# Layer 0's aggregate of panel 3: five of its seven products split a second time

## The chip, the cores and the metric

The kernel runs on one core of a Trainium2 chip. The metric is the device time of one execution in microseconds (us); the time given for a kernel is the median of several executions.

## What is computed

A graph with 2708 nodes of 1024 features goes through two attention layers. Cut to what matters here:

```
h = relu(layernorm(x))
# layer 0
f, g      = h @ Wf + bf, h @ Wg + bg
attention = softmax(where(adj > 0, relu(f @ g.T), NEG), axis=1)
x         = x + attention @ (h @ W + bW)
# layer 1: scores are leaky_relu(f1 + f2.T), the rest is alike
h         = relu(layernorm(x))
x         = x + relu(attention @ (h @ W))
```

All of it is in float32. The kernel forms `h.T @ attention.T` first (the aggregate, 1024 features by the nodes of a panel) and multiplies by W after that (the projection).

## The kernel before

**Panels.** The columns of the transposed attention are cut into five panels of 576, 576, 532, 512 and 512 nodes. The loop from L1768 on takes them one after the other through layer 0: `scores` (L1400) forms a panel's exponents' arguments, `project_q` (L701) prepares the right side of the next panel's scores, `aggregate` (L924) multiplies the rows of h by the panel's attention, and `project` (L1250) multiplies that by W. For the last two panels the order is shifted: the projection of panel 3 comes after the scores of panel 4 and before panel 4's aggregate. The loop from L1908 does the same in layer 1.

**The aggregate as seven products.** The 20 full row tiles are 10 pairs (`NQ`). Left and right side are seen as 2 by 2 blocks (the feature halves; the two tiles of a pair; the two halves of the panel), and seven block products M1 to M7 with sums of blocks on both sides take the place of eight. The left sums of layer 0 lie in DRAM as `hg_d` (made in `rows_h` and `sums_h`, L368 and L376); those of layer 1 lie in `hr_d` (`pair_h`). The right sums are made on VectorE in place: `T1`, `second`, `fourth` (L932 to L949). Each product is 40 matmuls of a 128x128 left block by half a panel, in `accumulate` (L665); in the trace each shows as two instructions, so 80 in all. The order is M1, M5, M2, M6, M3, M7, M4. The two left-over row tiles (`MONO`, `TINY`) have no partner and are added by `left_over` (L965) three times and by `into_m15` (L977) once.

**Split once more.** In layer 1, panels 1 to 4 use `aggregate_quartered` (L1087): each of the seven products is itself split into seven, over two pairs of tiles (`NK` = 5) and a quarter of the panel, so it becomes seven small products of 20 matmuls of 128x128 by a quarter panel. Their left sums of sums lie in `hs2_d`; `put_quarters` (L406) makes them: it reads 512 KB, makes four VectorE subtractions and additions of 256 columns, and writes 512 KB back. Their right sums are made by `make` (L1054): 20 VectorE instructions for one product, into five `quarter` tiles. The order is M1, M5, M2, M6, M7, M3, M4. A small product reads a `hc2` tile of 512 KB; two `hl2` tiles of 512 KB hold the last quarter-row of a product. The last small product of each product, M4 (`left_out`), is put off until after the first small product of the next.

**What sets the order of the work.** Loads go out on SyncE's queue in program order (`load`, L137). Stores and the reads of `put_quarters` go out on GpSimd's queue. VectorE work that isn't urgent is put into lists (`put`, L201): `later`, and `lazy` for work that only layer 1 needs. `behind(us)` (L214) is called at fixed places among the matmuls; it adds credit and takes items from `later`, and if that is empty and `spare[0]` is set also from `lazy`, until the credit is used up. An item's first number is what it costs in credit. When an item is taken, the loads of the next ones are put out too (`ahead`, L206). `spare[0]` is set during layer 0's aggregates of panels 1 to 4 (L1789), so layer 1's left sums of sums are made there. `accumulate` calls `behind(3.0)` four times in each product. What is not `held` is placed by the compiler's scheduler, which may move it among its engine's instructions.

**Where things are kept.** The pool `slots` has 54 buffers of up to 576 columns of float32: the panel's 22 attention tiles, the 14 tiles of the next panel's right side (`B`), `T1`, `quarter`, masks, the running maxima `mx` and others. The pool `strm` has 12 buffers of 4 KB for each partition: all tiles loaded on the fly (`hc`, `hc2`, `hl2`, `hq`, `As`, `w`, `adj_i`). [...] After the last product of an aggregate, GpSimd scales the result by the inverse sums (`scale`, L1019); the quartered form does it on VectorE (L1140).

Of the kernel before, what the change touches and what calls it, by code (L numbers as in the profile page):

```python
# [57 lines left out]
def kernel(  # L58
# [82 lines left out]
    def store(o, i):  # L141
        for a, b in in_16(o, i):
            nc.gpsimd.dma_start(a, b)  # L143
# [7 lines left out]


    hs_d = [dram.tile([P, 8, NH, P], FP, name=f"hs_d{q}") for q in range(NQ)]
    groups = [[q, q + 1] for q in range(0, NQ, 2)]
    group_of = {q: (i, j) for i, g in enumerate(groups) for j, q in enumerate(g)}
    assert sorted(group_of) == list(range(NQ))
    hg_d = [dram.tile([P, 7, len(g), W], FP, name=f"hg_d{i}") for i, g in enumerate(groups)]
    NK = NQ // 2
    WH = W // 2
    hr_d = dram.tile([P, 7, 2, 2, NK, WH], FP, name="hr_d")  # L160
    hs2_d = dram.tile([P, 7, 4, NK, WH], FP, name="hs2_d")

    def rows_at(m, q):

# [38 lines left out]

    def one(of=None):
        of = later if of is None else of
        for it in of[:4 if of is lazy and from_slots[0] else ahead[0]]:  # L206
            if it[1]:
                it[1]()
                it[1] = None
        us, _, go = of.pop(0)[:3]  # L210
        go()
        return us
# [154 lines left out]

    def rows_h(q, ha, hb):  # L368

        i, j = group_of[q]  # L370
        for m, h in ((M1, ha[0]), (M5, ha[1]), (M2, hb[0]), (M4, hb[1])):
            store(hg_d[i][:, m, j], h)

    summed, sums_may = [0], [True]

    def sums_h():  # L376

        def fetch(q, two):
            i, j = group_of[q]
            for m in (M1, M2):  # L380
                two.append(stream("hr", (P, 2, W)))
                (load if "m" in got else by_scalar)(two[-1], hg_d[i][:, m:m + 2, j])

        def first(q, two):
            (a0, a1), (b0, b1) = ((t[:, 0], t[:, 1]) for t in two)
            add(b1, a1, b1)
            sub(a1, a0, a1)

        def second(q, two):
            (a0, a1), (b0, b1) = ((t[:, 0], t[:, 1]) for t in two)  # L390
            sub(a0, b1, a0)
            sub(b0, b0, a0)
            i, j = group_of[q]
            store(hg_d[i][:, M6:M7 + 1, j], two[0])
            store(hg_d[i][:, M3, j], b0)
            store(hg_d[i][:, M5, j], b1)
            summed[0] += 1
        for q in range(NQ):
            two = []
            put(1.4, lambda q=q, two=two: held(first, q, two), lambda q=q, two=two: fetch(q, two), ready=lambda: sums_may[0])  # L400
            put(1.4, lambda q=q, two=two: held(second, q, two), ready=lambda: sums_may[0])

    BY_QUARTERS = (M1, M5, M2, M6, M7, M3, M4)
    made_quarters = {}

    def put_quarters(m, k, to=lazy):  # L406

        two = []

        def fetch():  # L410
            if from_slots[0]:
                two.extend(slot(f"hq{h}", (P, 2, WH)) for h in range(2))
            else:
                t = stream("hq", (P, 4, WH))
                two.extend(t[:, 2 * h:2 * h + 2] for h in range(2))
            for h in range(2):
                nc.gpsimd.dma_start(two[h], hr_d[:, m, h, :, k])

        def go():
            a11, a12, a21, a22 = (two[h][:, i] for h in range(2) for i in range(2))  # L420
            add(a22, a21, a22)
            sub(a21, a11, a21)
            sub(a11, a22, a11)
            sub(a12, a12, a11)
            for h in range(2):
                store(hs2_d[:, m, 2 * h:2 * h + 2, k], two[h])
            made_quarters[m] = made_quarters.get(m, 0) + 1
        put(1.7, go, fetch, to=to)

    def quarters_until(m):  # L430
        while made_quarters.get(m, 0) < NK:
            one(lazy if lazy else later)

    u = consts.tile([P, NC], FP, name="u")
# [489 lines left out]
    def aggregate(l, p, S, sm, then={}, rate=3.0):  # L924
# [26 lines left out]
        hc = {}  # L951

        order_of_products = (M1, M2, M4, M5, M6, M3, M7) if first else (M1, M5, M2, M6, M3, M7, M4)
        steps = [(m, i) for m in order_of_products for i in range(len(groups))]

        def left(m, q, d):
            i, j = group_of[q]
            at = steps.index((m, i))
            for m_, i_ in steps[at:at + (3 if l else 1)]:
                if (m_, i_) not in hc:  # L960
                    hc[m_, i_] = stream("hc", (P, 4, WH) if l else (P, 2, W))
                    load(hc[m_, i_], hr_d[:, m_, :, :, i_].rearrange("p h f c -> p (h f) c") if l else hg_d[i_][:, m_])
            return hc[m, i][:, d // 2 * 2 + j, d % 2 * P:(d % 2 + 1) * P] if l else hc[m, i][:, j, d * P:(d + 1) * P]

        def left_over(ps, e, s, start=False):  # L965
# [68 lines left out]
    def quarters_of(p, S):  # L1034
# [47 lines left out]
        def fourth():  # L1082
            for q in range(NQ):
                sub(t1(q), wb_(q)[:, lo], wa_(q)[:, lo])
        return {"make": make, "right": right, "first": first, "fifth": fifth, "second": second, "fourth": fourth}

    def aggregate_quartered(p, S, sm, of_right, then={}, fine=1.2):  # L1087

# [7 lines left out]
        lasts = {}  # L1098

        def product(m, n, ps, start):  # L1100
            quarters_until(m)
            if (m, 0) not in lasts:
                for i, of in enumerate((hr_d[:, m, :, :, NK - 1].rearrange("p h f c -> p (h f) c"), hs2_d[:, m, :, NK - 1])):
                    lasts[m, i] = stream("hl2", (P, 4, WH))
                    load(lasts[m, i], of)
            t = stream("hc2", (P, NK - 1, WH))
            raw = n in (M1, M2, M4)
            i = {M1: 0, M2: 1, M4: 3, M6: 0, M3: 1, M7: 2, M5: 3}[n]
            load(t, hr_d[:, m, i // 2, i % 2, :NK - 1] if raw else hs2_d[:, m, i, :NK - 1])
            last = lasts[m, int(not raw)][:, i]  # L1110
            for k in range(NK):
                for d in range(2):
                    lhs = t[:, k] if k < NK - 1 else last
                    nc.tensor.matmul(ps[:, d], lhs[:, d * P:(d + 1) * P], inner_right(m, n, k),  # L1114
                                     start=(start and k == 0 and d == 0), stop=(k == NK - 1), skip_group_check=True)
            behind(fine)
# [4 lines left out]
        def left_over(banks, e, s, fresh):  # L1121

            two = stream("hl", (P, W + 2 * P))
            load(two, hgl_d[1][:, e])
            cols = lambda b: slice(s.start + b * hb, s.start + (b + 1) * hb)
            for (a, b), ps in banks.items():
                for d in range(2):
# [41 lines left out]
        def with_second():  # L1169
# [2 lines left out]

        before_next = {M1: lambda: make(M5), M5: with_second, M2: lambda: (of_right["fourth"](), make(M6)), M6: lambda: make(M7),
                       M7: lambda: make(M3), M3: lambda: make(M4)}
        left_out = None
        for m in BY_QUARTERS:
            V = [quad(*direct[m])[:, 2 * r:2 * r + 2] for r in range(2)] if m in direct else [v[:, :, :h] for v in in_pairs("V")]
            c11, c12 = (V[0][:, :, b * hb:(b + 1) * hb] for b in range(2))
            c21, c22 = (V[1][:, :, b * hb:(b + 1) * hb] for b in range(2))
            X = bank2("gx")  # L1180
# [35 lines left out]
                into_place(m, V, 1)  # L1216
                scale(m, 1)
            if m == M5:
                of_right["second"]()
            if m == M5:  # L1220
                inverse.append(inverse_sums(p, sm))
            if m in then:
                then[m]()
        left_out()
# [354 lines left out]
    def rows_done(t, xt):  # L1579
# [14 lines left out]
        if panel_of[t] == NP - 1:  # L1594
# [18 lines left out]
            else:  # L1613
# [14 lines left out]
                (held if last else call)(rest[0])  # L1628
                put_max(1, q)
                if q == NQ - 1:  # L1630
                    for m in BY_QUARTERS:
                        put_quarters(m, q // 2, later)
                    for p in range(2, NP):
                        for s in (NQ - 2, NQ - 1):
                            put_max(p, s, lazy)
# [11 lines left out]
        if whole and q == LEFT:  # L1647
            put(0.0, lambda: left_h(1, *(done_rows[s] for s in mine)))
            put(0.0, met)
        elif whole:  # L1650
            put(2.7, lambda: pair_h(q, *(done_rows[s] for s in pairs[q])))
            put(0.0, met)
            quads_met[q // 2] = quads_met.get(q // 2, 0) + 1
            if quads_met[q // 2] == 2:
                put(0.0, lambda: [put_quarters(m, q // 2) for m in BY_QUARTERS])

    def halves_of_tiny(name):
        t = slot(name)[:, :2 * P].rearrange("p (e j) -> p e j", e=2)
# [7 lines left out]
        return list(full(p)) + ([MONO, TINY][p - 1:p] if p in (1, 2) else [])  # L1666

    ORDERED = (NP - 1,)

    def by_gpsimd(o, i, **k):  # L1670
        tc.keep_in_program_order(nc.gpsimd.dma_start(o, i, **k))
# [96 lines left out]
    for p in range(NP):  # L1768
# [18 lines left out]
            then[M6] = lambda: first_masks(NP - 1, 1)  # L1787
            then[M7] = lambda: first_masks(NP - 1, 2)
        spare[0], from_slots[0] = p > 0, p == NP - 1  # L1789
        G[p] = aggregate(0, p, S, got["sm"], then)  # L1790
        spare[0] = False
        if p == 0:
            flush()
            ahead[0] = 2
            for s in range(1, NP):
                columns_to_row(r_d[s], s, r_[:, first_col[s]:])
            spread_wa()
# [110 lines left out]
    for p in range(NP):  # L1908
# [3 lines left out]
            then = dict(zip((M2, M6) if p else (M3, (M7, "middle")), (lambda p=p: take_shifts(p + 1), lambda p=p: take_weights(p + 1))))  # L1912
        spare[0] = p < 2
        ahead[0] = 2 if p else 4
        g = aggregate_quartered(p, S, sm, next_right, then, fine=1.0) if p else aggregate(1, p, S, sm, then, rate=4.0)
        hooks = {}
        if p + 1 < NP:
            next_right = quarters_of(p + 1, got["P"][0])
# [31 lines left out]
```

## Time and profile before

| what | us |
|---|---|
| median of 3 executions | 3048.35 (3043.93 to 3048.83) |
| the profiled execution | 3049.19 |
| its span | 3047.3 |
| TensorE matmul busy | 2993.9 |
| TensorE weight load busy | 2294.2 |
| VectorE busy | 2047.6 |
| ScalarE busy | 536.8 |
| GpSimd busy | 496.9 |
| DMA | 766.78 MB, mean 252 GB/s |

All times of single instructions come from that one profiled execution, on a clock that starts with its span. PE is TensorE's matmul, PEld its weight load, DVE is VectorE, ACT ScalarE, POOL GpSimd, SP SyncE, SPq SyncE's DMA queue. Names such as `hc<-hg_d` are output and input of an instruction, with buffer numbers left out (so `hs_d` stands for `hs_d` and `hs2_d`, `hc` for `hc` and `hc2`, `hl` for `hl` and `hl2`). Almost all VectorE instructions have line L45, that of a helper. An instruction's duration overlaps with the next one's start, so a pace is read from the difference of two starts. Times in parentheses or brackets after a row are the idle time before it and what ended it.

### The profile page before, as it was taken

How to read it: one execution, taken by the hardware profiler on the slowest of the kernel's cores; microseconds unless marked ns; L12 is line 12 of the kernel's file. 1: busy time of each engine (PE TensorE's matmuls, PEld its weight loads, DVE VectorE, ACT ScalarE, POOL GpSimd, SP SyncE). 2: the span in 40 equal slices, each digit the busy share in tenths (PEclk: the TensorE clock that was granted, in tenths of full speed). 3: DMA queues.
4: the chain of work that ended last, by engine and by line, in shares of the span. 5: the costliest groups of instructions: out<-in, count | busy, mean ns of one | idle time of the engine just before them, and what ended most of it. 6: DMA issues, size and time to landing. Idle time of an engine off the chain costs nothing.

```text
span 3047.3 us, 41722 instructions
## 1 busy us (share of the span) xinstructions
PE 2993.9 (98%) x14642; PEld 2294.2 (75%) x14642; DVE 2047.6 (67%) x4667; ACT 536.8 (18%) x880; POOL 496.9 (16%) x770
## 2 busy tenths in 40 slices
PE   8998999999999999999999999999999999999999
PEld 4576777667877588885888886784767959879695
DVE  5776794585742686616965276867878768887863
ACT  4420020020200121101210111302232121212200
POOL 1421111210112110223111111131212010020201
PEclk9999999999999999999999999999999999999999
DMA  6989878887466786768957588679768768878887
GB/s 232 302 271 272 311 276 308 264 286 235 133 236 165 228 273 195 247 156 251 292 188 251 179 241 258 223 292 335 245 212 264 263 202 299 294 265 297 264 294 268
DMA packets 392704, 766.78 MB, mean 252 GB/s; under 512 B 65728, under 2 KB 206944, under 8 KB 392464
## 3 DMA queue, kind: packets, MB, share of 16 engines
q1 hardware_dynamic: 332336, 584.80, 59.6%
q0 software_dynamic: 54464, 164.78, 16.1%
q10 hardware_dynamic: 5696, 14.55, 1.4%
q8 instruction: 116, 1.90, 0.2%
q14 instruction: 92, 0.75, 0.1%
HBM read 630.04 MB, written 138.11 MB: 252 GB/s over the span
## 4 chain that ended last, share of the span: by engine, by line
PE 73%; DVE 11%; issue 8%; DMA 5%; POOL 1%; ACT 1%; SPq 1%; POOLq 0%; DVEq 0%; ACTq 0%
PE sz L1425 6%; PE gy L679 6%; PE gz L679 6%; PE gz L1114 5%; PE gx L679 5%; PE sx L1425 4%; PE pz L1314 4%; PE sy L1425 4%; PE px L1314 4%; PE py L1314 3%; PE gy L1114 3%; PE gx L1114 3%; PE gv L679 3%; PE M_ps L591 3%; PE qz L679 2%
## 5 line engine op out<-in xcount | busy, mean ns | idle before, releaser
L1425 PE MATMUL sz<-B,As 128*128 128x288 f32 (+2 forms) x1200 | 292.0, 392 | 6.0 <-DVE st L45 5.1
L1425 PEld LDWEIGHTS sz<-B,As 128*128 128x128 f32 x1200 | 227.2, 190 | 55.2 <-DVE st L45 8.4
L1425 PE MATMUL sx<-B,As 128*128 128x288 f32 (+2 forms) x800 | 200.8, 394 | 12.4 <-DMA As<-hs_d 10.4
L1425 PE MATMUL sy<-B,As 128*128 128x288 f32 (+2 forms) x800 | 199.0, 392 | 0.0
L1425 PEld LDWEIGHTS sx<-B,As 128*128 128x128 f32 x800 | 152.5, 191 | 45.8 <-DMA As<-hs_d 9.5
L679 PE MATMUL gz<-Sa,hc 128*128 128x288 f32 (+2 forms) x800 | 185.8, 392 | 0.0
L679 PEld LDWEIGHTS gz<-Sa,hc 128*128 128x128 f32 x800 | 151.5, 190 | 32.2 <-issue 2.2
L1425 PEld LDWEIGHTS sy<-B,As 128*128 128x128 f32 x800 | 151.7, 190 | 30.6 <-DVE st L45 0.3
L1114 PE MATMUL gz<-quarter,hc 128*128 128x128 f32 (+2 forms) x1344 | 168.8, 279 | 3.8 <-DVE gT L45 3.7
L1114 PEld LDWEIGHTS gz<-quarter,hc 128*128 128x128 f32 x1344 | 160.6, 191 | 5.1 <-DVE gT L45 4.6
L143 POOL DMA_DIRECT2D out_dram<-x_res x164 | 81.2, 502 | 469.1 <-DVE x_res L45 461.9
L1314 PE MATMUL py<-w,ps 128*128 128x512 f32 x320 | 142.0, 593 | 0.0
L1314 PE MATMUL pz<-w,ps 128*128 128x512 f32 x320 | 142.0, 594 | 0.0
L1314 PE MATMUL px<-w,gT 128*128 128x512 f32 x320 | 141.1, 593 | 0.0
L679 PE MATMUL gy<-T,hc 128*128 128x288 f32 (+2 forms) x480 | 114.9, 402 | 3.8 <-DMA hc<-hg_d 3.8
L1314 PEld LDWEIGHTS pz<-w,ps 128*128 128x128 f32 x320 | 60.2, 190 | 76.2 <-issue 72.2
L1314 PEld LDWEIGHTS py<-w,ps 128*128 128x128 f32 x320 | 60.5, 190 | 75.1 <-issue 72.7
L591 PE MATMUL M_ps<-wgT,wfT 128*128 128x512 f32 x256 | 112.7, 596 | 1.6 <-ACT hsT L45 1.6
L1314 PEld LDWEIGHTS px<-w,gT 128*128 128x128 f32 x320 | 60.1, 190 | 71.3 <-issue 67.8
L679 PEld LDWEIGHTS gy<-T,hc 128*128 128x128 f32 x480 | 93.1, 194 | 24.7 <-DMA hc<-hg_d 4.3
L143 POOL DMA_DIRECT2D mk_d<-mask x55 | 35.9, 654 | 456.4 <-DVE mask L45 439.4
L45 ACT ACTIVATE P<-P 128x576 f32<-128x576 f32 (+3 forms) x111 | 72.1, 650 | 207.3 <-DVE P L45 207.2
(391 smaller groups left out, 5819.6 us busy)
## 6 DMA issues: line engine op xcount, KB each, us to landing
hc<-hg_d SPq DMA_DIRECT2D x175, 512.0 KB
As<-hs_d SPq DMA_DIRECT2D x150, 512.0 KB
hc<-hr_d SPq DMA_DIRECT2D x119, 512.0 KB
hc<-hs_d SPq DMA_DIRECT2D x112, 512.0 KB
w<-wt_d SPq DMA_DIRECT2D x96, 512.0 KB
w<-in_L_gnn_W_dram SPq DMA_DIRECT2D x72, 512.0 KB
md<-md_d SPq DMA_DIRECT2D x56, 512.0 KB
adj_i<-in_adj_dram SPq DMA_DIRECT2D x200, 128.0 KB
```

The costliest lines, as they stand in the source:

```text
L45: i = f(*a, **k)
L143: nc.gpsimd.dma_start(a, b)
L591: nc.tensor.matmul(ps, wfT[a][c // NH][:, c % NH, :], wgT[b][c], start=(c == 0), stop=(c == NC - 1))
L679: nc.tensor.matmul(ps[d], left(m, k, d), right(m, k), start=(start and k == 0), stop=(k == K - 1), skip_group_check=True)
L1114: nc.tensor.matmul(ps[:, d], lhs[:, d * P:(d + 1) * P], inner_right(m, n, k), start=(start and k == 0 and d == 0), stop=(k == NK - 1), ski ...
L1314: nc.tensor.matmul(ps, left[i][m][:, k, :], w_[k], start=(start and k == 0), stop=(k == NH - 1), skip_group_check=True)
L1425: nc.tensor.matmul(ps[:n, :h], lefts[q][:, i % 2, c, :n], B[m][c // 2][:, c % 2, :h], start=(start and c == 0), stop=(c == NH - 1), skip_g ...
```

## The change

Panel 3 of layer 0 takes `aggregate_quartered` too, with M1 and M5 left as they were and only M2, M6, M7, M3 and M4 split again. Around it:

- `hg_d` becomes one DRAM tensor in place of five, and `hs2_d` two, one for each layer.
- `put_quarters` gets a layer. For layer 0 it reads 512 KB from `hg_d` with one DMA on GpSimd's queue into a `hq` tile, costs 4.0 in credit (layer 1: 1.7), and is not held. 35 such items (five products by five quarter-rows) are put into `lazy` after panel 0's aggregate, ahead of all of layer 1's.
- When a lazy item is taken, the loads of the first three items of the list, itself included, are put out (it was two in the aggregates of panels 1 to 3).
- In panel 3, M1 and M5 run through `accumulate`; M1's result is copied twice by ScalarE straight into the result's tiles; the right sums for M2 are made in the middle of M5, the sums' inverses after M5. The results of the five split products are collected in a `V` tile of the pool `strm`, added in place by VectorE and scaled by VectorE.
- After each small product `behind(1.2)` is called. The hooks of the panel (`first_masks` of panel 4) hang on M2, M6 and M7 as before.

```diff
-    groups = [[q, q + 1] for q in range(0, NQ, 2)]
...
-    hg_d = [dram.tile([P, 7, len(g), W], FP, name=f"hg_d{i}") for i, g in enumerate(groups)]
+    hg_d = dram.tile([P, 7, NK, 2, W], FP, name="hg_d")
...
-    hs2_d = dram.tile([P, 7, 4, NK, WH], FP, name="hs2_d")
+    hs2_d = [dram.tile([P, 7, 4, NK, WH], FP, name=f"hs2_d{l}") for l in range(2)]
...
-        for it in of[:4 if of is lazy and from_slots[0] else ahead[0]]:
+        for it in of[:(4 if from_slots[0] else 3) if of is lazy else ahead[0]]:
...
-    BY_QUARTERS = (M1, M5, M2, M6, M7, M3, M4)
+    BY_QUARTERS = ((M2, M6, M7, M3, M4), (M1, M5, M2, M6, M7, M3, M4))
...
-    def put_quarters(m, k, to=lazy):
+    def put_quarters(l, m, k, to=lazy):
...
         def fetch():
+            if l == 0:
+                t = stream("hq", (P, 2, 2, WH))
+                nc.gpsimd.dma_start(t.rearrange("p f h c -> p f (h c)"), hg_d[:, m, k])
+                two.extend(t[:, :, h] for h in range(2))
+                return
...
             for h in range(2):
-                store(hs2_d[:, m, 2 * h:2 * h + 2, k], two[h])
-            made_quarters[m] = made_quarters.get(m, 0) + 1
-        put(1.7, go, fetch, to=to)
+                store(hs2_d[l][:, m, 2 * h:2 * h + 2, k], two[h])
+            made_quarters[l, m] = made_quarters.get((l, m), 0) + 1
+        put(1.7 if l else 4.0, go, fetch, to=to)
...
-    def aggregate_quartered(p, S, sm, of_right, then={}, fine=1.2):
+    def aggregate_quartered(l, p, S, sm, of_right, then={}, fine=1.2, rate=3.0):
...
         def product(m, n, ps, start):
-            quarters_until(m)
+            quarters_until(l, m)
             if (m, 0) not in lasts:
-                for i, of in enumerate((hr_d[:, m, :, :, NK - 1].rearrange("p h f c -> p (h f) c"), hs2_d[:, m, :, NK - 1])):
+                rows = hr_d[:, m, :, :, NK - 1] if l else hg_d[:, m, NK - 1].rearrange("p f (h c) -> p h f c", h=2)
+                for i, of in enumerate((rows, hs2_d[l][:, m, :, NK - 1])):
                     lasts[m, i] = stream("hl2", (P, 4, WH))
...
-            load(t, hr_d[:, m, i // 2, i % 2, :NK - 1] if raw else hs2_d[:, m, i, :NK - 1])
+            load(t, hs2_d[l][:, m, i, :NK - 1] if not raw else hr_d[:, m, i // 2, i % 2, :NK - 1] if l else
+                 hg_d[:, m, :NK - 1, i % 2, i // 2 * WH:(i // 2 + 1) * WH])
...
+        def sums_of_columns():
+            of_right["second"]()
+            inverse.append(inverse_sums(p, sm))
+
+        def collected():
+            if l == 0:
+                t = stream("V", (P, NH, h))
+                return [t[:, 2 * r:2 * r + 2, :h] for r in range(2)]
+            return [v[:, :, :h] for v in in_pairs("V")]
+
+        if l == 0:
...
+            def first_product(d, ps):
+                nc.scalar.copy(quad(0, lo)[:, d], ps)
+                nc.scalar.copy(quad(1, lo)[:, d], ps)
+            exps_until(NQ)
+            of_right["fifth"]()
+            accumulate(left, of_right["operand"], NQ, h, (M1, M5), then,
+                       {M1: first_product, M5: lambda d, ps: add(quad(0, hi)[:, d], ps, quad(0, lo)[:, d])}, "g",
+                       {M5: sums_of_columns}, rate=rate, by_k=True, more={(M5, NQ // 2): with_second})
+
         left_out = None
-        for m in BY_QUARTERS:
+        for m in BY_QUARTERS[l]:
...
+    SPLIT_EARLY = (3,)
...
-        G[p] = aggregate(0, p, S, got["sm"], then)
+        if p in SPLIT_EARLY:
+            G[p] = aggregate_quartered(0, p, S, got["sm"], quarters_of(p, S), then)
+        else:
+            G[p] = aggregate(0, p, S, got["sm"], then)
         spare[0] = False
         if p == 0:
+            for m in BY_QUARTERS[0]:
+                for k in range(NK):
+                    put_quarters(0, m, k)
             flush()
```

## The prediction

> **What bounds the kernel now.** I read the page first, then TensorE's waits, then the busy time by stretches, then TensorE's instructions in order of time in two aggregates of the same width, then the DMA slices of one aggregate, then single rows of VectorE's.
>
> ```profile
> PE 2993.9 (98%) x14642; PEld 2294.2 (75%) x14642; DVE 2047.6 (67%) x4667; ACT 536.8 (18%) x880; POOL 496.9 (16%) x770
> ```
>
> TensorE is the bound. Its waits add up to some 48 us in the whole span, and in layer 0's aggregates of panels 1, 2 and 3 it has none. So a microsecond of matmul that is taken out there is a microsecond of the end, as long as nothing else becomes late. The stretches say how much room the others have. Columns: stretch, its length, then busy time of PE, PEld, DVE, ACT, POOL, the clock, DMA share, GB/s. They are layer 0's aggregates of panels 1, 2 and 3, and layer 1's quartered aggregate of panel 3, which has the same width of 512:
>
> ```profile
> 838.80:987.00 148.20, 148.20 (x630) 114.24 (x629) 47.80 (x110) 6.05 (x13) 27.82 (x28) 1.00 0.67 200
> 1236.00:1373.00 137.00, 137.00 (x629) 114.07 (x628) 44.94 (x110) 4.46 (x11) 29.70 (x34) 1.00 0.69 208
> 1610.50:1742.50 132.00, 132.00 (x630) 114.16 (x629) 47.21 (x117) 11.14 (x16) 20.42 (x21) 1.00 0.72 223
> 2698.00:2823.50 125.50, 123.20 (x1127) 121.51 (x1126) 100.56 (x285) 22.89 (x43) 4.87 (x10) 1.00 0.88 300
> ```
>
> In layer 0 VectorE idles for two thirds and the DMA engines for 30%. The quartered form takes 125.5 us in place of 132.0, with VectorE at 80% and DMA at 0.88: it is cheaper for TensorE and dearer for all others.
>
> **The gain, from TensorE's rows.** First the plain form in panel 3 of layer 0: M2 with its left-overs, then the last rows of M4 and the first of what follows.
>
> ```profile
> 1644.92 13.98 PE L679 MATMUL gx<-Sb,hc 128*128 128x256 f32 x64
> 1658.73 1.89 PE L971 MATMUL gx<-Sa,hl 128*128 128x256 f32 x8
> ...
> 1661.20 3.72 PE L679 MATMUL gx<-Sb,hc 128*128 128x256 f32 x16
> 1664.76 17.43 PE L679 MATMUL gz<-Sa,hc 128*128 128x256 f32 x80
> 1682.02 13.98 PE L679 MATMUL gy<-Sb,hc 128*128 128x256 f32 x64
> ...
> 1742.39 1.89 PE L1425 MATMUL sx<-B,As 128*128 128x256 f32 x8
> ```
>
> A product is 1682.02 - 1664.76 = 17.26 us (80 by 0.216); left-overs are 1661.20 - 1658.73 = 2.47. Then the quartered form in layer 1:
>
> ```profile
> 2743.06 1.95 PE L1114 MATMUL gy<-P,hc 128*128 128x128 f32 x16
> 2744.85 0.61 PE L1114 MATMUL gy<-P,hl 128*128 128x128 f32 x4
> 2745.30 0.61 PE L1129 MATMUL gx<-P,hl 128*128 128x128 f32 x4
> ...
> 2800.95 0.71 PE L1129 MATMUL gz<-P,hl 128*128 128x128 f32 x4 [1.15 <-DVE V L45]
> ```
>
> A small product is 2745.30 - 2743.06 = 2.24 us (20 by 0.112), seven are 15.65; left-overs are 2.53. So a split product saves 17.26 - 15.65 = 1.6 us, five save 8.1, and four left-overs take back 4 x 0.06 = 0.2: **7.9 us gross**. As a check, the five products of layer 1's panel 3 ran from 2729.66 to 2823.30 = 93.6 us; without a small product of M5 (2.2) and transposes for the next panel (1.4) that is 90.0, against 1742.39 - 1644.92 = 97.5 less 0.9 for the sums = 96.6 here. That gives 6.6, with the 1.15 us wait of the last row above in it, so 7.7 without. I take 7.7.
>
> [...] The trace's pace of 112 ns and PEld at 121.5 of 125.5 us agree: the small matmuls run at the pace of their weight loads, [...]. [...] 128 columns go at a pace of 0.20 us and 256 at 0.34, not half. [...] where the DMA runs at over 400 GB/s below, TensorE indeed doesn't wait.
>
> **Part by part.**
>
> *35 new sums in panels 1 and 2.* Each costs four VectorE instructions and 1.05 MB of DMA. VectorE's pace is read here (the seven items of layer 1 in panel 3), the DMA's room in the slices of panel 1's aggregate (40 slices of 3.7 us):
>
> ```profile
> 1619.32 8.46 DVE L45 TENSOR_TENSOR hq<-hq 128x256 f32<-128x256 f32 x25
> DMA  8655999999965446445434445453444475869999
> GB/s 228 194 149 154 326 372 395 409 415 413 422 206 140 136 132 169 108 132 136 139 101 134 137 142 142 142 163 94 136 142 142 142 227 146 195 135 177 275 232 242
> ```
>
> VectorE: 35 x 4 x 8.46/25 = 47 us, into 193 us of idle time in these two aggregates. Credit: 4 x 7 calls of 3.0 make 84 in each; about one call goes to the last exponentials. At 4.0 an item that is some 20 items in panel 1 and the other 15 in panel 2, one for every 17.26 x 4/12 = 5.8 us (a little more at their greater width). The DMA then has 140 GB/s (the floor, `hc` alone) plus 1.05 MB / 5.8 us = 181: 321 GB/s, below the 410 it reaches. VectorE can be late here: PSUM of M5 and M6 isn't needed again for a product (17 us), that of M3 for half of one (8.6). GpSimd issues one load and two stores an item, some 2 us in 5.8. I cost this at nothing; without that cover an item that is late by its 4 to 7 us landing would cost TensorE that minus 8.6, still nothing. Bounds 0 to 3, taken 0.3. Two or three of the 12 stream buffers stay taken through the scores between; `As` loads were issued 29 us before use (1713 for 1742), so losing a quarter of that is hidden.
>
> *Layer 1's sums move back.* 14 items come behind the 35: about 12 at the end of panel 2's aggregate, the others in panel 3's M1 and M5, with the 7 that were there. On GpSimd's queue each is four DMAs of 0.71 us, 2.8 us in 2.5 us of pace: the queue is full for 30 us. Behind it stand the scaling of the result (4.7 and 2.4 us, needed at 1373 and finished at 1355: 18 us of cover) and the bias loads for the projection. Bounds 0 to 10, taken 0.
>
> *Panel 3 itself.* Loads: nine of 512 KB for a split product in place of five, 4.7 MB in 15.65 us = 301 GB/s, as in layer 1, where no wait on a load shows. Besides, panel 4's `adj_i` loads stand on the same queue (eight at 1640 take 7.6 us of it), and two `adj_i`, `V`, two to four `hl2` and an `hl` leave four or five of 12 buffers for `hc2`, four by 2.24 = 9 us ahead. No row shows this. A gain is excluded, as there is no load wait to lose; bounds 0 to 4 (each of two mask steps once late by half its 4 us transfer), taken 1.0.
>
> VectorE: `make` is 20 instructions by 0.20 = 4.0 us (the chain of waits has 18 in 3.64), 20 us for five; evictions, additions in place and scaling some 28 where 11 fall away: 47 + 20 + 17 = 84 of 125 us, below layer 1's 100.6. Its lateness at the left-overs (the wait in the row at 2800.95) showed 2.2, 1.2, 1.2 and 0 us in layer 1's four panels: taken 1.1, bounds 0 to 2.2. The inverse (3.4 us) delays nothing in layer 1 either. ScalarE's four extra copies (0.37) and GpSimd's vanished scaling (7.1) are beside.
>
> Buffers: attention 22, `B` 14, `T1` 5, `mx` 4, inverse and sum 2 are 47 of 54; one set of `quarter` is 5, masks up to 3. So the next product's `quarter` tiles partly wait until `left_out` has read the last ones, one for each 0.45 us, and `make` needs 0.8 us a tile: TensorE comes to the first some 2 us later, the fifth is late by about 0.7. Three times that is 2; bounds 0 to 4, taken 1.0, as some are free.
>
> **Sum:** -7.7 + 1.1 + 1.0 + 1.0 + 0.3 = **-4.3 us**. The profiled execution (3049.2) would be 3044.9; it lies 0.8 above the median of 3048.35, so I forecast **3044.0**. `hg_d` as one tensor adds nothing if stores and loads of different parts aren't ordered against each other.
>
> **Rivals.** (1) *All is hidden*: only the 7.7 counts: 3040.6. For it: layer 1's panel 4 had no wait in these products. Against it: layer 1 has no `B` in its buffers. Chance 0.15. (2) *Slower, by late right sums*: `quarter` for the next product is made only after the last one's end, so at four changes of product TensorE waits for all of `make`, 4.0 us: -7.7 + 16 = +8.3, 3056.7. It decides from 7.7/4 = 1.9 us a change on. For it: the count of 47 + 5 + 3 of 54. Against it: layer 1 makes 22 new tiles meanwhile without this. Chance 0.22. (3) *It doesn't do what it says*: `later` eats the credit, ten of the 35 sums are left and forced at panel 3's products, one after the other by their 2.5 us of stores: +25 - 7.7, 3065. The margin is five items of credit. Chance 0.08. The forecast has 0.55, from 3040 to 3048.5.
>
> **From that the numbers.** 0.2%, 6.1 us, is about what can be told from no change. Faster by over that: 0.15 of the forecast's share and rival 1: 0.30. Within: 0.38 of the forecast and 0.04 of the others: 0.42. Slower: 0.02 + 0.20 + 0.06 = 0.28. The range is 3038.5 (7.7 gained and 2 of scatter) to 3058 (rival 2).
>
> **What would show it.** Right: the five products take 92 to 94 us in place of 96.6, no wait in panels 1 and 2, `V` waits of 1 to 2 us. Wrong: TensorE waiting for `quarter` (rival 2), `hq` work in panel 3 for layer 0 (rival 3), a wait for `gT` at the start of panel 2's projection (GpSimd's queue), waits for `hc` in panel 0 (`hg_d`) or 3.

## The result, and the profile after

| kernel | median, us | lowest to highest | profiled execution | its span |
|---|---|---|---|---|
| before | 3046.27 (4 executions) | 3043.93 to 3048.83 | 3049.19 | 3047.3 |
| after | 3082.89 (4 executions) | 3079.71 to 3091.20 | 3079.84 | 3077.8 |

The ratio after to before is 1.0119, 95% interval 1.0104 to 1.0134. The kernel became slower by some 37 us; the forecast was 3044.0 and the range ended at 3058. The two spans differ by 30.5 us.

First TensorE's waits in the whole span (what waits, what it waits for: total, times, longest). The list is close to that of before, with one large entry on top:

```profile
PE sum_ps L903 <- DVE gT L45: 35.0, 1, 35.0
PE sx L1458 <- DMA As<-hs_d: 9.6, 1, 9.6
```

Then the three stretches that the prediction showed, layer 0's aggregates of panels 1, 2 and 3, with the same columns:

```profile
837.90:1023.20 185.30, 150.28 (x629) 115.30 (x628) 76.00 (x174) 6.04 (x13) 56.67 (x73) 0.91 0.72 242
1272.10:1409.00 136.90, 136.90 (x629) 114.02 (x629) 58.88 (x145) 4.79 (x11) 59.08 (x74) 1.00 0.82 277
1645.60:1770.00 124.40, 124.10 (x985) 118.53 (x984) 82.83 (x246) 8.48 (x22) 13.35 (x19) 1.00 0.92 303
```

Panel 3 did what it was to do: 124.4 us in place of 132.0, VectorE at 82.8 (84 was worked out), DMA at 303 GB/s (301). Panel 2 is unchanged. Panel 1 takes 185.3 in place of 148.2: +37.1. With the 7.6 gained in panel 3 that makes 29.5 of the 30.5 between the spans; 1.0 is left for all the rest. The DMA's share there is 0.72, so it isn't full.

TensorE's row at that place, before (without a wait) and after:

```profile
941.36 1.13 PE L903 MATMUL sum_ps<-sm,ones 128*128 128x288 f32 x4
...
975.74 2.29 PE L903 MATMUL sum_ps<-sm,ones 128*128 128x288 f32 x4 [35.02 <-DVE gT L45]
```

M3 ended at 940.7 (975.74 - 35.02). VectorE takes a product's results out of PSUM, which is called its eviction here. The next matmul, of the sums for the inverse, waited 35.02 us for the eviction of M3 (`gT<-gy,u`). VectorE's rows, first that of before, then those after from 928 to 976, tell why it came 35 us late. In the brackets: idle time before the row, and what ended it.

```profile
938.65 0.46 DVE L45 TENSOR_TENSOR gT<-gy,u 128x288 f32<-128x288 f32 x1 [18.87 <-PE gy L679]
...
930.95 1.80 DVE L45 TENSOR_TENSOR hq<-hq 128x256 f32<-128x256 f32 x4 [5.16 <-DMA hq<-hg_d]
943.96 1.80 DVE L45 TENSOR_TENSOR hq<-hq 128x256 f32<-128x256 f32 x4 [11.20 <-DMA hq<-hg_d]
945.68 1.54 DVE L45 TENSOR_TENSOR u<-gz,m 128x288 f32<-128x288 f32 x4
950.51 1.80 DVE L45 TENSOR_TENSOR hq<-hq 128x256 f32<-128x256 f32 x4 [3.29 <-DMA hq<-hg_d]
964.71 1.80 DVE L45 TENSOR_TENSOR hq<-hq 128x256 f32<-128x256 f32 x4 [12.39 <-DMA hq<-hg_d]
973.52 1.80 DVE L45 TENSOR_TENSOR hq<-hq 128x256 f32<-128x256 f32 x4 [7.01 <-DMA hq<-hg_d]
975.24 1.18 DVE L45 TENSOR_TENSOR gT<-gy,u 128x288 f32<-128x288 f32 x3
```

In the row of before the eviction waits for its product, and for nothing else. After, each row of four `hq<-hq` is one new sum. There are 25 of them (five products by five), 23 in panel 1; the text before the result has 35. VectorE isn't busy: it stands before each sum for its load. The evictions of M6 (`u<-gz,m`) and M3 stand behind these sums in VectorE's order, have nothing to do with them, and take 1.5 us once it is their turn. GpSimd's queue in the same time shows what the loads were late for:

```profile
946.78 0.55 POOL L408 DMA_DIRECT2D hq<-hg_d  x1
951.69 0.71 POOL L143 DMA_DIRECT2D hs_d<-hq  x1 [4.37 <-DVE hq L45]
952.61 0.72 POOL L143 DMA_DIRECT2D hs_d<-hq  x1 [0.21 <-issue]
960.95 0.55 POOL L408 DMA_DIRECT2D hq<-hg_d  x1 [7.62 <-DMA hs_d<-hq]
965.89 0.71 POOL L143 DMA_DIRECT2D hs_d<-hq  x1 [4.38 <-DVE hq L45]
966.81 0.72 POOL L143 DMA_DIRECT2D hs_d<-hq  x1 [0.21 <-issue]
969.84 0.55 POOL L408 DMA_DIRECT2D hq<-hg_d  x1 [2.31 <-DMA hs_d<-hq]
```

One round: load at 946.78, sum at 950.51 (3.7 us later), stores at 951.69 and 952.61, and the next load only when these stores have landed, at 960.95. In the compiled program, ten of the 23 loads of panel 1 name as their condition the two stores of an earlier sum, because they take over its stream buffer; in the trace ten loads waited 45.5 us in all for such stores. Of loads 18 to 22, four take over the buffer of the sum just before, and these sums follow the one before them at 9 to 14 us. And VectorE's compiled order has 11, 18 and 21 sums ahead of the evictions of M5, M6 and M3, where e3 below, with the sums held in program order, has 8, 11 and 14: what isn't held was moved forward.

From 848.9, when the first sum began, to 975.3 are 21 sums at 6.0 us on average. Up to the end of M3 there was time for 15 of them (91.8 / 6.0). This gives a way to take the wait apart: **wait = sums ahead x us for each - the time until the product ends.** In the run from which the us for each are taken it only restates what was measured; the experiments change its factors.

### The profile page after: what moved, and what is told of

Same layout as the page of the kernel before. It is cut to its first block, busy times and chain, and to the rows that moved or that the text cites. A ratio compares the mean times of both kernels' runs of the same rounds, so it can differ in the third digit from the quotient of the medians.

```text
span 3077.8 us, 42914 instructions
## 1 busy us (share of the span) xinstructions
PE 2990.7 (97%) x15006; PEld 2301.9 (75%) x15006; DVE 2125.2 (69%) x4896; ACT 539.8 (18%) x890; POOL 539.8 (18%) x843
## 4 chain that ended last, share of the span: by engine, by line
PE 53%; DVE 10%; DMA 2%; issue 2%; ACT 1%; POOL 1%; SPq 0%; DVEq 0%; POOLq 0%
PE gz L1120 6%; PE gx L1120 4%; PE gy L1120 4%; PE sz L1458 4%; PE pz L1347 4%; PE px L1347 4%; PE gy L679 4%; PE py L1347 3%; PE gz L679 3%; PE gx L679 3%; PE sx L1458 2%; PE sy L1458 2%; DVE P L45 2%; PE gv L679 2%; PE qz L679 1%
## 5 line engine op out<-in xcount | busy, mean ns | idle before, releaser
L1120 PE MATMUL gz<-quarter,hc 128*128 128x128 f32 (+2 forms) x1584 | 198.2, 278 | 3.8 <-DVE gT L45 3.7
L1120 PEld LDWEIGHTS gz<-quarter,hc 128*128 128x128 f32 x1584 | 188.6, 191 | 5.2 <-DVE gT L45 4.6
L45 DVE TENSOR_TENSOR hq<-hq 128x256 f32<-128x256 f32 x212 | 86.6, 434 | 120.1 <-DMA hq<-hg_d 78.5
L679 PE MATMUL gz<-Sa,hc 128*128 128x288 f32 (+2 forms) x640 | 151.6, 397 | 0.0
L679 PEld LDWEIGHTS gz<-Sa,hc 128*128 128x128 f32 x640 | 121.9, 191 | 28.3 <-issue 1.8
```

Of the source, the lines that this page charges most:

```text
L45: i = f(*a, **k)
L679: nc.tensor.matmul(ps[d], left(m, k, d), right(m, k), start=(start and k == 0), stop=(k == K - 1), skip_group_check=True)
```

## The experiments

All rows compare with runs of the kernel before on the same chip. "Ahead" counts the sums ahead of M3's eviction in panel 1, "taken over" the loads in panel 1 that take over a stream buffer from the stores of an earlier sum, by the compiled program. "Pool of 54" means that the sums' tiles lie in the pool `slots` and not in a stream buffer.

| run | edit to the changed kernel | ahead | taken over | wait at M3, us | median, us | ratio to before, 95% |
|---|---|---|---|---|---|---|
| after | none | 21 | 10 of 23 | 35.0 | 3082.89 | 1.0104 to 1.0134 |
| e1 | panel 3 not split | 21 | as after | 36.4 | 3089.49 | 1.0117 to 1.0150 |
| e2 | no new sums | 0 | 0 | 0 | 3043.90 | 0.9974 to 0.9988 |
| e3 | sums held | 14 | 3 of 23 | 0 | 3059.64 | 1.0019 to 1.0045 |
| e4 | pool of 54 | 17 | 0 | 0 | 3045.28 | 0.9979 to 0.9995 |
| e5 | both | 14 | 0 | 0 | 3048.81 | 0.9980 to 1.0004 |
| e6 | held, one buffer | 12 | all | 30.5 | 3146.45 | 1.0290 to 1.0336 |
| e7 | credit 6.0 | 15 | 3 of 16 | 0.4 | 3085.02 | 1.0103 to 1.0135 |
| e8 | loads on SyncE | 21 | 7 of 23 | 22.0 | 3069.33 | 1.0051 to 1.0087 |
| e11 | pool of 54, credit 6.0 | 12 | 0 | 0 | 3081.21 | 1.0080 to 1.0117 |
| e13 | pool of 54, credit 3.0 | 24 | 0 | 13.0 | 3074.95 | 1.0047 to 1.0101 |
| e14 | all sums in the pool of 54, 6.0 | 12 | 0 | 0 | 3077.69 | 1.0053 to 1.0096 |

(The expectations of e3 and e7 speak of some seventeen and some twelve loads that wait in the changed kernel; it is ten, in the trace too.)

**Which part costs: e1 and e2.** The change cut in two.

```diff
-    SPLIT_EARLY = (3,)
+    SPLIT_EARLY = ()
```

> The 25 new sums are made in panels 1 and 2, but panel 3 keeps the plain aggregate, so nothing reads them. Theory A (the sums alone cost the time, in panel 1's aggregate): TensorE waits there 30 to 38 us for gT, and the time is the changed kernel's plus the 7 us that the split products save, some 3087 to 3092. Rival B (the wait comes from the two parts together): no wait in panel 1, 3046 to 3050.

```profile
PE sum_ps L903 <- DVE gT L45: 36.4, 1, 36.4
```

Theory A, within its range: the sums alone cost all. The 40.5 us over before, less the 5 to 6 that e2 below gains, are close to the 36.6 of the whole change.

```diff
-                    put_quarters(0, m, k)
+                    pass
...
-            quarters_until(l, m)
+            if l:
+                quarters_until(l, m)
...
-            load(t, hs2_d[l][:, m, i, :NK - 1] if not raw else hr_d[:, m, i // 2, i % 2, :NK - 1] if l else
+            load(t, hs2_d[l][:, m, i, :NK - 1] if l and not raw else hr_d[:, m, i // 2, i % 2, :NK - 1] if l else
...
```

> Panel 3 is split as in the change, but the 25 new sums are left out, and the small products M5, M6, M7 and M3 read blocks of the sums' sources in place of the sums of sums (so layer 0's panel 3 has other numbers in it; the loads have the same sizes). Theory A: the part is a gain by itself, 96.6 us become 89 to 90, the whole 3038 to 3042. Rival B (the split costs elsewhere, or the layer 1 sums that are made in panels 1 to 3 are what wait): 3047 or more.

Measured 3043.9, ratio 0.9981: 5.8 us faster than before by the ratio, 5.1 by the medians. The split is the gain that the prediction gave it, within the interval (3.7 to 7.9), and 3043.9 was just above what was expected.

**Order or buffer: e3, e4, e5.**

```diff
-        put(1.7 if l else 4.0, go, fetch, to=to)
+        put(1.7 if l else 4.0, go if l else lambda: held(go), fetch, to=to)
```

> Only change: VectorE's four instructions of a new sum are held in program order. Ahead of the evictions of M5, M6 and M3 in panel 1 there stand 8, 11 and 14 items in place of 11, 18 and 21, and three loads in place of some seventeen wait for the landing of an earlier item's stores. Theory A (order and reused buffers): an item isn't asked for before its place, the wait of 35 us shrinks to 0 to 8 us, 3040 to 3050. Rival C (the items are simply too dense for GpSimd's queue and the DMA: 16 items or more by some 7 us each in that aggregate): the last of them are still late, wait 15 us or more, 3060 to 3083.

```profile
914.41 0.46 DVE L45 TENSOR_TENSOR u<-gz,m 128x288 f32<-128x288 f32 x1 [12.60 <-PE gz L679]
917.70 5.22 DVE L45 TENSOR_TENSOR hq<-hq 128x256 f32<-128x256 f32 x12
936.65 0.46 DVE L45 TENSOR_TENSOR gT<-gy,u 128x288 f32<-128x288 f32 x1 [13.73 <-PE gy L679]
```

Now the evictions wait for their products, and three sums run through without a gap. 21 sums, two fewer than in the changed kernel, were made in this aggregate or just after it, so it was not too dense for GpSimd's queue or the DMA (its share was 0.78 in panel 1), and C falls. But the whole is 11 us slower than before, not faster, and that no theory had foretold. The first of TensorE's waits says where:

```profile
PE py L1347 <- DMA w<-wt_d: 10.9, 1, 10.9
```

And the waits of SyncE's queue between 930 and 1025 say why:

```profile
SPq L139 <- DMA hs_d<-hq: 21.1, 5, 7.5
```

The sums' tiles are stream buffers too until their stores have landed. SyncE's loads of `hc` took them over and waited 21.1 us for that (none in the kernel before), so the first load of weights for the projection went out at 966.6 and not at 946.4, and those from `wt_d` came 10.9 us late. It is the same wait for a landing, felt by another queue.

```diff
-                t = stream("hq", (P, 2, 2, WH))
-                nc.gpsimd.dma_start(t.rearrange("p f h c -> p f (h c)"), hg_d[:, m, k])
-                two.extend(t[:, :, h] for h in range(2))
+                two.extend(slot(f"hq{h}", (P, 2, WH)) for h in range(2))
+                for h in range(2):
+                    nc.gpsimd.dma_start(two[h], hg_d[:, m, k, :, h * WH:(h + 1) * WH])
```

> Only change: a new sum's 512 KB lie in two buffers of the pool of 54 (two loads of 256 KB on GpSimd's queue in place of one of 512 KB), not in a stream buffer; the sums are not held, and 13, 17 and 21 items stand ahead of the evictions of M6, M3 and the left-overs. Theory A1 (what makes an item late is its load, which waits for the landing of the stores of the item before in the same stream buffer): wait of 0 to 5 us in panel 1, 3040 to 3047. Rival A2 (the order alone decides, an item that is moved ahead of an eviction delays it whatever its buffer): 13 and 17 items ahead still cost 15 us or more, 3060 to 3075. Rival C (GpSimd's queue): now 4 DMAs an item in place of 3, so later still, 3083 or more.

3045.28, ratio 0.9987: faster than both kernels. M3's eviction is on time though 17 sums stand ahead of it, with four DMAs for each on GpSimd's queue, at 291 GB/s:

```profile
930.48 0.42 DVE L45 TENSOR_TENSOR hq<-hq 128x256 f32<-128x256 f32 x1 [4.56 <-DMA hq<-hg_d]
930.94 0.88 DVE L45 TENSOR_TENSOR hq<-hq,hq 128x256 f32<-128x256 f32 x2
931.86 0.42 DVE L45 TENSOR_TENSOR hq<-hq 128x256 f32<-128x256 f32 x1
939.65 0.46 DVE L45 TENSOR_TENSOR gT<-gy,u 128x288 f32<-128x288 f32 x1 [7.37 <-PE gy L679]
```

So A1 holds at this number of sums, and A2 and C don't. In the pool of 54 a load takes over a buffer now and then too, but the wait is small: two loads waited 4.4 us in all for landings, against the 45.5 us of ten in the changed kernel. (This edit also halves the loads; e3 and e6 differ in the buffers with loads of 512 KB in both.)

> Both edits of the two runs before: the new sums lie in the pool of 54 and are held in program order. Theory A (late loads through reused stream buffers made the items late, and the stream buffers that the held form kept through the start of the projection made its weights late): neither wait is left, all that is gained in panel 3 shows, 3038 to 3043. Rival (the pool of 54 is short of buffers in panel 1, so the attention tiles or the next panel's right side come late): 3046 or more, with waits on VectorE in panel 1 or 2.

Neither wait is left in panel 1 or its projection, as A had it, but the ratio 0.9992 can't be told from 1 nor from e4's. Loads of layer 0's `hc` show two waits of 1.8 us in all in panel 2. Holding adds nothing to e4.

**The round trip by itself: e6, and by another queue: e8.**

```diff
-    strm = ctx.enter_context(tc.tile_pool(name="strm", bufs=12))
+    strm = ctx.enter_context(tc.tile_pool(name="strm", bufs=11))
+    own = ctx.enter_context(tc.tile_pool(name="own", bufs=1))
...
-                t = stream("hq", (P, 2, 2, WH))
+                t = own.tile([P, 2, 2, WH], FP, tag="own", name="hq")
...
-        put(1.7 if l else 4.0, go, fetch, to=to)
+        put(1.7 if l else 4.0, go if l else lambda: held(go), fetch, to=to)
```

> Held as before, but every one of the 25 new sums goes through one buffer of its own (the stream pool has 11 in place of 12), so each load waits for the landing of the stores of the item before. Theory A (the round trip of load, sum and landing is what makes items late, 9 to 14 us each in the changed kernel's panel 1): 12 items stand ahead of M3's eviction, 12 by 9 to 14 from 848 on is 956 to 1016 where 940 is needed, so TensorE waits 15 to 75 us in panel 1 and more for the items after; 3075 to 3160. Rival B (held order is enough, whatever the buffers): 3058 as with the stream buffers, or less.

```profile
PE sum_ps L904 <- DVE gT L45: 30.5, 1, 30.5
PE px L1348 <- issue: 18.2, 1, 18.2
```

With the sums held as in e3, and every load behind the landing of the sum before, the wait is back, and the start of the projection stands for another 18.2. From 869.4 to 991.3 there are twelve sums, 122 / 11 = 11 us from one to the next: inside the 9 to 14 read from the changed kernel. Rival B falls: order is not enough. (Some 20 us of this kernel's loss lie ahead of panel 1, which begins at 858; their cause wasn't sought. The stream pool is smaller by one buffer here, which may have its part in the total, but the new sums' loads don't use it.)

```diff
-                nc.gpsimd.dma_start(t.rearrange("p f h c -> p f (h c)"), hg_d[:, m, k])
+                load(t.rearrange("p f h c -> p f (h c)"), hg_d[:, m, k])
```

> Only change to the changed kernel: the loads of the new sums go out on SyncE's queue, in program order, not on GpSimd's. VectorE's order is exactly that of the changed kernel (11, 18, 21 and 23 items ahead of the evictions of M5, M6, M3 and the left-overs). Seven of 23 loads wait for the stores of an earlier item; the loads of the products stand behind them. Theory A (loads held up by stores, on GpSimd's queue and in its buffers): wait of 0 to 15 us in panel 1, with some on hc; 3040 to 3062. Rival A2 (VectorE's order decides): 30 us or more as before, 3078 to 3090.

22.0 us, between the two. VectorE's order is that of the changed kernel, so its 35.0 isn't set by the order alone; there are 21 sums from 848.6 to 962.0, 5.4 us each in place of 6.0. Fewer loads take over a buffer here, and they stand on another queue; this run doesn't separate the two. SyncE's queue, which has the products' loads too, stood behind landings of sums' stores for 82.2 us from 838 to 962, and for 86.0 in the changed kernel (none in e4), and in neither did TensorE wait for a load of `hc` in panel 1.

**Number ahead: e13**, which puts the number back up without the stream buffers.

```diff
-        put(1.7 if l else 4.0, go, fetch, to=to)
+        put(1.7 if l else 3.0, go, fetch, to=to)
```

> The new sums in the pool of 54, not held, at 3.0 in credit in place of 4.0: 9, 17, 24 and 28 items stand ahead of the evictions of M5, M6, M3 and the left-overs in panel 1, as many as in the changed kernel (11, 18, 21, 23) or more, all new sums and the first of layer 1's among them. Theory A1 (the reused stream buffer decides): wait on an eviction of 0 to 8 us in panel 1, 3040 to 3053. Rival A2 (the number ahead decides): 20 us or more, 3062 to 3085.

```profile
916.53 1.54 DVE L45 TENSOR_TENSOR u<-gz,m 128x288 f32<-128x288 f32 x4
...
945.24 2.60 DVE L45 TENSOR_TENSOR hq<-hq 128x256 f32<-128x256 f32 x6 [7.52 <-DMA hq<-hr_d]
947.75 0.45 DVE L45 TENSOR_TENSOR gT<-gy,u 128x288 f32<-128x288 f32 x1
```

The wait lies between the two expectations. In e4 M6's eviction begins 16.7 us after the product does. Here, with 17 sums ahead, it comes 6.4 us later than that, which costs nothing; in the changed kernel, with 18 ahead, it comes 30.1 us later. One sum more is worth some 4 of the 24 us between them; the rest goes with the buffers. The 13.0 us at M3 come with the number, as e4 differs from this run in the credit alone: 24 sums at 4.2 us (101.7 / 24) where e4 has 17. They aren't pure, though: in the row at 945.24 VectorE stands 7.5 us for the load of a sum of layer 1, in a stream buffer still, which went out at 938.7, behind the stores of the sum before. So both factors of the formula count. In e3 and e4 they weren't changed quite apart: e3's order also leaves fewer loads that take over a buffer, and e4 also has fewer sums ahead. By the formula 21 sums at 4.2 us, 88 us, would have fitted into the 91.8 of the changed kernel (an estimate; no run has just that). A wait of 10.3 us for `w<-wt_d` followed, as in e3.

**Spacing: e7, e11, e14.** Only the credit was changed in e7, from 4.0 to 6.0.

> Only change to the changed kernel: a new sum costs 6.0 in credit in place of 4.0; not held, stream buffers. 16 of the 25 fall into panel 1 and nine into panel 2; 9, 13 and 15 stand ahead of the evictions of M5, M6 and M3, and three loads of panel 1 wait for stores alone in place of some twelve. Theory A: 13 items at 7 us from 848 on end at 939, 15 at 953, where 918 and 940 are needed, if the round trip is what paces them; as few loads wait for stores it is less: wait of 0 to 12 us, 3040 to 3053. Rival D (density is not it, the hoisting by itself is): some 15 us or more of wait, 3060 or more.

In panel 1 it went as A said (0.4 us). But the median is that of the changed kernel: the nine sums that moved to panel 2 met layer 1's there.

```profile
1344.03 2.14 PE L903 MATMUL sum_ps<-sm,ones 128*128 128x266 f32 x4 [16.68 <-DVE gT L45]
1422.02 9.09 PE L1347 MATMUL py<-w,ps 128*128 128x512 f32 x16 [18.00 <-DMA w<-wt_d]
```

The wait was moved by a panel, not removed.

> The new sums in the pool of 54, not held, at 6.0 in credit in place of 4.0. Theory A: with the wait for landings gone, spacing has nothing left to mend: within 3 us of the run at 4.0, 3043 to 3048. Rival D (density itself costs, through GpSimd's queue and the DMA): at least 3 us less than at 4.0, under 3041; or more time, from the nine sums that then fall into panel 2 beside layer 1's (wait there as with the stream buffers, 3055 or more).

A was wrong: 8.5 us at M3 in panel 2 and 18.1 for `w<-wt_d`. Layer 1's sums still used stream buffers there (SyncE's queue waited 44.5 us for landings of their stores between 1335 and 1440). Hence e14, with these in the pool of 54 too.

> All sums of both layers in the pool of 54, not held, the new ones at 6.0 in credit. With only the new ones there, panel 2 and the start of its projection had waits of 8.5 and 18.1 us. Theory A1 (layer 1's items, whose loads took over stream buffers, were what came late there, and the weights stood behind their stores): both waits fall to 0 to 5 us together, 3045 to 3057. Rival D (16 items of the two layers beside each other are too dense for GpSimd's queue, whatever the buffers): 15 us or more of wait, 3065 or more.

The wait at M3 is gone, so that one was the buffers. The other fell only to 15.2, and panel 3's aggregate took 138 us. SyncE's queue from 1335 to 1425:

```profile
SPq L139 <- POOL x_res L1692: 12.8, 1, 12.8
```

A load that SyncE issues ahead of the weights waited for a memset on GpSimd, which stands behind the sums' loads and stores there (it ran at 1389). So for this wait rival D's queue is right: the fuller GpSimd queue at the end of this aggregate delayed what the projection loads, by these 12.8 us on SyncE's queue. What made panel 3 longer wasn't followed; 6.4 us of it are one wait at its first split product.

**Further with it: e12, e9, e10.** All on top of e4: layer 1's sums of panels 1 to 3 moved to the pool of 54; panel 4 split too; panels 2 and 4.

> The new sums in the pool of 54, not held, at 4.0, and layer 1's sums of panels 1 to 3 moved there too, so that no sum takes a stream buffer. SyncE's queue stood 53.6 us behind stores of sums in the kernel before and 77.3 us in the run with only the new sums moved. Theory A (that queue's stands are still hidden, as TensorE doesn't wait for a product's load there): within 3 us of the run with only the new sums moved, 3041 to 3048. Rival E (the stands cost time that shows as scattered small waits): 3 us or more faster, under 3041; or, if the pool of 54 runs short in panel 3, slower, 3049 or more.

Ratio 1.0008 (0.9999 to 1.0017), median 3052.98 beside 3050.87 before: nothing is won, so E's gain falls, and it is a little slower than e4. That fits E's other branch, the pool of 54 short in panel 3: TensorE waits there 3.0 us for `V` and 1.0 for `gT`, and in e4 0.2 in all.

> The form with the new sums in the pool of 54 (not held), and panel 4's aggregate of layer 0 split in the same way as panel 3's; it reads the same sums of sums, so no new sum is made for it. Theory A (what the split gives in panel 3, some 7 us, it gives wherever VectorE and the loads keep up, and the price is in making the sums alone): another 4 to 7 us over the run with the sums in that pool, 3034 to 3041. Rival: panel 4's aggregate has the last of layer 1's sums and of its own masks on VectorE, and the pool of 54 is fuller, so right sums or evictions come late: 3045 or more with waits on VectorE after 1870.

Slower than before: 1.0038 (1.0023 to 1.0052). Panel 4's own aggregate went from 131 to 129 us, but layer 1's first aggregate from 152 to 171:

```profile
PE gy L679 <- DMA hc<-hr_d: 15.6, 3, 11.2
```

Its loads waited on SyncE's queue for stores of layer 1's sums (37.0 us at the longest): VectorE's instructions for these sums in panel 4 went from 28 to none, and in layer 1's first aggregate from 28 to 56. The rival's sign was right, its place wrong.

> As the run with panels 3 and 4, and panel 2 (532 wide) split as well. The 25 sums are due from 1270 on; 23 of them are made in panel 1's aggregate. Theory A: another 4 to 7 us, 3028 to 3037. Rival: in panel 2 layer 1's sums, the two last new ones and the masks of panel 3 stand on VectorE, which goes from 59 to over 95 us of work in 137: waits on VectorE or on loads of 5 us or more, 3037 to 3050.

1.0131 (1.0109 to 1.0152). Panel 2 took 147 us in place of 137, with 5.8 us of waits for loads and 6.5 for right sums (4.0 at the longest, the size of rival 2 in the prediction), and `w<-wt_d` was 13.0 late. Of the panels tried, the split paid in panel 3 alone.

## Why the prediction was wrong

- **The gain: right.** "I take 7.7" stands against 1682.41 to 1771.70 for panel 3's five products, 89.3 us for 96.6: 7.3 net of all of panel 3's own costs. The whole panel gives 7.6.
- **Panel 3's costs: too high, together 3.1 for about 0.4.** No wait for V (1.1 taken), one load wait of 0.3 us on `hc<-hg_d` (1.0 taken), no wait for `quarter` (1.0 taken). Rival 2, with the count of 47 + 5 + 3 of 54 buffers, did not occur there.
- **Layer 1's sums and GpSimd's queue: right for the changed kernel** (no `hq` work forced in panel 3, the scaling of panel 2's result in time), so rival 3 didn't occur. In e14, with more sums in panel 2, the projection's wait was 15.2, beyond the bound of 10.
- **`hg_d` as one tensor: right**: the wait for it in panel 0 is 4.0 us, 3.8 before.
- **The failing step** is "I cost this at nothing; without that cover an item that is late by its 4 to 7 us landing would cost TensorE that minus 8.6, still nothing. Bounds 0 to 3, taken 0.3". It measured 37 us. Three things are wrong in it. It lets one sum be late by one landing of its load; but VectorE ran its work in the compiled order, so a sum that waited held what stood behind it (12.39 us at 964.71 and 7.01 at 973.52, with M3's eviction behind both), and ten loads waited 45.5 us for the *stores* of an earlier sum, so the lateness added up. It has the sums one for each 5.8 us in the program's places, whereas they weren't held and 18 stood ahead of M6's eviction, not 11. (That the mean of 6.0 us is close to 5.8 is chance: the one is what the waits came to, the other the pace of the credit.) And the cover of 8.6 us after M3 wasn't there: the matmul of the sums comes right behind M3 and waited for its eviction, so TensorE stood for 35.0 us from M3's end on. The line "Two or three of the 12 stream buffers stay taken" was about the scores between; who takes over a sum's buffer within the aggregate was not asked.
- The prediction and the text before it say 35 new sums, five products by five; that is 25. The trace has 25 loads, 23 of them for panel 1. The sum of VectorE's work was so overestimated (47 us for 34), which made no difference to the error; that 23 and not 20 came into panel 1 was small beside it.

What the prediction named as the sign of being wrong was not what came: it looked to panel 3 and to GpSimd's scaling, and had "no wait in panels 1 and 2" only as a sign of being right.

The 4 to 7 us for a landing held in the median: the new sums' loads took 4.4 us to landing in the median (3.7 in the round above), and the stores 4.5 in panel 1 and 6.4 over the whole trace. The round is longer: in the one above the next load went out 8.3 us after the second store was issued (960.95 - 952.61). And a load that waited held its queue: in the 7.62 us before the row at 960.95 GpSimd issued nothing else, and in e3 the loads of `hc` that waited 21.1 us on SyncE's queue had the first load of weights behind them, which went out at 966.6 and not at 946.4.

## What to carry to other kernels

Work that is put "beside" a critical engine is priced by its round trip through the buffer it uses (load, work, store, landing; 11 us in e6), times the number of such items that stand ahead of the next critical instruction in its engine's compiled order (21 ahead of M3's eviction here); compare that product with the time there is, not one item's lateness with one gap. Ask for each new transfer whose buffer it takes over and who takes over its own, in every queue, and look at the compiled order for what isn't held. Spacing such work out is no cure by itself: here it moved the wait to the next panel (16.7 us at M3 there in e7).

## What the runs showed of the hardware

After the wait of 35 us TensorE came back slow: the four instructions of `sum_ps` took 2.29 us. They took 1.13 before, and in e7, after a wait of 0.4, 1.24 at the same width:

```profile
937.77 1.24 PE L903 MATMUL sum_ps<-sm,ones 128*128 128x288 f32 x4 [0.39 <-DVE gT L45]
```

The stretches around the wait, with the columns as above, show the granted clock (the third number from the end):

```profile
925.00:940.70 15.70, 15.70 (x70) 11.51 (x68) 2.46 (x6) 0.00 (x0) 3.75 (x6) 1.00 0.68 230
944.00:948.00 4.00, 0.00 (x0) 0.00 (x0) 3.12 (x8) 0.00 (x0) 1.98 (x3) 0.70 0.32 131
948.00:975.70 27.70, 0.00 (x0) 0.00 (x0) 5.48 (x14) 0.00 (x0) 4.75 (x8) 0.50 0.63 222
978.10:980.00 1.90, 1.90 (x6) 1.29 (x6) 1.90 (x2) 0.00 (x0) 0.55 (x1) 0.58 0.10 19
980.00:990.00 10.00, 10.00 (x43) 7.85 (x42) 6.18 (x5) 0.41 (x1) 7.01 (x4) 1.00 0.37 128
```

A mean of 0.70 over 944 to 948 is one half from 945.6 on, and a mean of 0.58 over 978.1 to 980 is one half until 979.7. So here the clock fell to one half 4.9 us after M3's end and rose again 4.0 us after TensorE had restarted. 4.0 us at half speed lose 2.0 (an estimate), and panel 1's matmul busy time went from 148.2 to 150.3: the long wait cost about 2 us beyond itself.
